# A four-layer graph attention kernel: the last layer's output stores move from SyncE's queue to ScalarE's

## The chip, the cores and the metric

The kernel runs on one core of a Trainium2 chip. The metric is the time of one execution on the device in microseconds (us). The core has five engines with a queue of instructions each: TensorE (PE, its weight loads shown apart as PEld), VectorE (DVE), ScalarE (ACT), GpSimd (POOL) and SyncE (SP). A transfer (DMA) is issued by one of these queues and then carried by the core's 16 DMA engines. A queue runs its instructions in order: one that waits holds up everything behind it.

## The reference

Four layers follow one another. Each adds the result of a graph attention to its input and normalises every row. There are 4096 nodes with 256 features; the adjacency matrix is random with density 1/256, plus the diagonal. The first three layers take a softmax over each row's neighbours. The last one, which the change touches, takes two:

```python
h = x @ W                                           # layer 3
e = leaky_relu(h @ a[:256] + (h @ a[256:]).T, 0.2)
att = softmax(where(adj > 0, e, -1e12), axis=1)
neg = -softmax(where(adj > 0, -e, -1e12), axis=1)
new = concatenate([att @ x, neg @ x], axis=1) @ fc_W
x = layernorm(x + elu(new))                         # the output
```

## The kernel before

The rows are worked in tiles of 128, so a layer has 32 tiles. A first part of the program turns each tile's adjacency into 13 lists of at most 128 neighbour nodes and a mask for each list. A layer then needs no full matrix: for each tile POOL gathers 13 blocks of 128 rows of `vals` (here: the features, already multiplied by the halves of `fc_W`, and two logarithms of attention terms) by index, `G<-vals,idx` at L645. The fourteenth block is the tile's own rows. It needs no index and comes by SP's queue: `G<-vals` at L642. A block is 128 x 516 floats, 258 KB.

A tile is worked in two halves of seven blocks (`RowTile.half`, L649). In layer 3 a half is: seven Relus on ACT that add the row's and the neighbours' terms (L686), an exponential (L687), its product with the mask on DVE (L688), a second exponential from the same Relus (L689), its product with the mask (L690), and 28 matrix products on PE (L723) that add into two banks. The own-row block belongs to the first half, at its seventh place (`FRONT = 6`).

Four of the 32 tiles, number 28 to 31, are worked densely against all nodes (`whole_rows`, L948): ACT makes the attention terms `pw` (L985, L987, L989), DVE masks them (L990), PE multiplies them by blocks `vw` (L993). This work is cut into units that are strewn between the halves of the 28 other tiles. It makes two passes over the nodes, one for each softmax; the second begins at about 1930 us.

`half_with_whole` writes one step of this weave: half a tile, then in the first half of tile m the finish of tile m-1, then some units of dense work. `finish` (L1060) reads the two banks: `positive` (L1050) scales the first with a reciprocal (L1054 on DVE, L1057 on ACT, giving `z`), L1074 to L1082 add the second, the elu's exponential (L1080 on ACT) and the old row `y`. `norm` (L1015) takes mean and variance (L1022, L1023), the reciprocal root by a chain of small DVE instructions (L1031 to L1041), and scales `y` (L1043). `GROUPS` says that the 28 gathered tiles are normalised alone and the four dense ones together. A tile's row block `y` is loaded by SP (`load_x`, L1012) into one of nine buffers, is changed in place, and is stored from the same buffer (L1045). A new `y` that takes the buffer waits until the store has landed.

The order on each engine is fixed when the program is built. A scheduler places the instructions by its own estimate of times; `issue_after(ins)` makes what is written inside it stand behind `ins`. So SP's queue in layer 3 holds, in a fixed order: a tile's row terms `S` (L635), its masks `mk` (L637), a finished row block's store (L1045), the own-row block of a coming tile (L642), its `y` (L1012), and the dense work's `vw` and `mw` (L970, L968). Buffers of `G` come from two pools of 16 and 14, shared by all tiles.

The end of the program is `close` with no following layer: what is left of the dense work, and the finish of the last tile.

Of the kernel before, what the change touches and what calls it, by code (L numbers as in the profile page):

```python
# [44 lines left out]
AF = mybir.ActivationFunctionType  # L45
# [5 lines left out]
P = 128  # L51
# [129 lines left out]
class Turns:  # L181


    def __init__(self, pools):
        self.pools = list(pools)
# [418 lines left out]
class RowTile:  # L604
# [44 lines left out]
    def half(self, half):  # L649
        L, n, nc = self.layer, self.layer.n, self.layer.nc  # L650
        prog, sh, S = L.prog, L.shared, self.S
        H, Wd, V, T, A = HEADS[n], WIDTH[n], VALS[n], TERMS[n], LOGS[n]
        if self.accs is None:
            pool = prog.ptwo[1 if n == 3 and self.step % 2 else 0]
            self.accs = [prog.bank(pool) for _ in range(2 if n == 3 else 1)]
        accs = self.accs
        G = [self.place(half * HALF + k) for k in range(HALF)]
        mh = self.mk[:, half * HALF:(half + 1) * HALF, :]
        if n < 2:

            if prog.masks is None:
                prog.masks = prog.bank(prog.pmask)
            there = prog.masks[:, half * BANK // 2:half * BANK // 2 + HALF * P // 4].bitcast(I32)
            nc.vector.tensor_scalar(there.rearrange("p (t i) -> p t i", t=HALF),
                                    mh.rearrange("p t i -> p (t i)").bitcast(I32)
                                    .rearrange("p (t i) -> p t i", t=HALF)[:, :, :P // 4], 0, None,
                                    op0=ALU.bitwise_or)
            mh = there.bitcast(U8)
            mh2 = mh.rearrange("p (o i) -> p o i", o=1).to_broadcast([P, 2, HALF * P])
        else:  # L670
            mh = mh[:, :, :P]
        pairs = [prog.wp.tile([P, 2, HALF, P], F32, name="w") for _ in range(H // 2)]
        w = [pair[:, k] for pair in pairs for k in range(2)]
        if n < 2:
            w = [w[1], w[2], w[3], w[0]]
        def masked(pair):

            pair = pair.rearrange("p h t i -> p h (t i)")
            nc.vector.scalar_tensor_tensor(pair, pair, LEAST, mh2, op0=ALU.max, op1=ALU.mult)  # L679

        def d(k, h):
            return G[k][:, V + T + h:V + T + h + 1]

        if n == 3:
            for k in range(HALF):
                nc.scalar.activation(w[0][:, k, :], S[:, 0, :], AF.Relu, bias=d(k, 0))  # L686
            nc.scalar.activation(w[1], w[0], AF.Exp, scale=-1.0)  # L687
            nc.vector.tensor_tensor(w[1], w[1], mh, op=ALU.mult)  # L688
            nc.scalar.activation(w[0], w[0], AF.Exp, bias=sh["shift2"])  # L689
            nc.vector.tensor_tensor(w[0], w[0], mh, op=ALU.mult)  # L690
            heads = (1, 0)
        else:
            for h in range(A, T):
                k = 0
                while k < HALF:
                    pos = half * HALF + k
                    e = 2 if pos % 2 == 0 and k + 1 < HALF else 1
                    if e == 2:
                        dd = self.slots[pos // 2][:, :2 * ROW[n]].rearrange("p (t c) -> p t c", t=2)
                        nc.vector.tensor_tensor(  # L700
                            w[h][:, k:k + 2, :], S[:, h:h + 1, :].to_broadcast([P, 2, P]),
                            dd[:, :, V + T + h:V + T + h + 1].to_broadcast([P, 2, P]), op=ALU.mult)
                    else:
                        nc.vector.tensor_scalar(w[h][:, k, :], S[:, h, :], d(k, h), None, op0=ALU.mult)
                    k += e
            for h in range(A):
                for k in range(HALF):
                    nc.scalar.activation(w[h][:, k, :], S[:, h, :], AF.Exp, bias=d(k, h))  # L708
                if n == 2:
                    nc.vector.scalar_tensor_tensor(w[h], w[h], LEAST, mh, op0=ALU.max, op1=ALU.mult)  # L710
                elif h % 2 == 0:
                    masked(pairs[h // 2])
            heads = list(range(A, H)) + list(range(A))
        for h in heads:
            for k in range(HALF):
                pos = half * HALF + k
                how = dict(start=pos == 0 and (n == 3 or h == heads[0]), stop=pos == NP - 1, skip_group_check=True)
                v = G[k][:, h * Wd:(h + 1) * Wd]
                if n < 2:
                    nc.tensor.matmul(accs[0][:Wd, h * P:(h + 1) * P], v, w[h][:, k, :], **how)  # L720
                else:
                    a = accs[h][:, :Wd] if n == 3 else accs[0][:, h * Wd:(h + 1) * Wd]
                    nc.tensor.matmul(a, w[h][:, k, :], v, **how)  # L723
# [22 lines left out]
class Layer:  # L746
# [3 lines left out]
    def __init__(self, prog, n):  # L750
        self.prog, self.n, self.nc, self.shared = prog, n, prog.nc, prog.shared
        self.order = ORDER[n]
        self.count = len(self.order)
        self.tiles = {}
        self.loaded = set()
        self.units = self.whole_rows()
        self.total = len(WHOLE[n]) * NT * (1 if n < 3 else 2)
        self.used = self.ahead = 0
        self.nxt = self.middle = self.between = None
        self.stored = []  # L760
        self.group = []
        self.ready = []
        self.step = 0
        self.last = ()
# [7 lines left out]
    def load(self, m, half):  # L772
        if m < self.count and (m, half) not in self.loaded:
            self.loaded.add((m, half))
            self.tile(m).load(half)
# [63 lines left out]
    def half_with_whole(self, m, part):  # L839

        projs = []
        self.step = 2 * m + part

        able = sorted((e for e in self.ready if e[0] < self.step), key=lambda e: e[2] >= MIX)
        self.set_banks()

        over = self.used == self.total and m > self.count - 4
        for entry, banks in zip(able, (self.prog.banks, self.prog.pthree)[:1 + over]):
            self.ready.remove(entry)
            projs.append(Projection(self.prog, self.n + 1, self.nxt, *entry[1:], banks=(banks,) * 3))  # L850
            projs[-1].transpose()
        with ExitStack() as order:
            for ins in self.last:
                order.enter_context(self.prog.tc.issue_after(ins))
            self.last = ()
            if part == 1 or self.tile(m).accs is None:
                self.tile(m).half(part)
        if self.between is not None:

            self.last = self.between()  # L860
            self.between = None
        for proj in self.stored:
            proj.store()
        for proj in projs:
            proj.copy()
            proj.multiply()
        if part == (0 if self.n == 3 else 1) and m >= 1:
            self.tile(m - 1).finish()
        self.whole(2 * m + part)
        for proj in projs:  # L870
            proj.row()
            proj.edge()
        self.stored = projs

    def steps(self):
        for m in range(self.count):
            for part in range(2):
                self.part(m, part)
# [10 lines left out]
    def close(self, following):  # L889
# [16 lines left out]
        if WHOLE[self.n]:  # L906
            for _ in self.units:
                pass
            if following is None:
                self.tile(last).finish()  # L910
                return


# [101 lines left out]
    def norm(self, y, m):  # L1015


        nc, ep = self.nc, self.prog.ep
# [22 lines left out]
            nc.vector.tensor_tensor(r, r, u, op=ALU.mult)  # L1041
        for i, (y, m) in enumerate(self.group):
            self.scaled = nc.vector.tensor_scalar(y, y, mv[:, i, 0:1], r[:, i:i + 1], op0=ALU.subtract, op1=ALU.mult)  # L1043
            dst = self.prog.out if self.n == 3 else self.shared["x"][self.n + 1]
            nc.sync.dma_start(out=dst[m * P:(m + 1) * P, :], in_=y)  # L1045
            if self.n < 3:
                self.ready.append((self.step + 1, y, m))
        self.group = []

# [38 lines left out]
def dense_layers(ctx: ExitStack, tc: tile.TileContext, ins: dict, out: bass.AP, ident):  # L1088
# [361 lines left out]
    def layer(nodes, following):  # L1450
        n = nodes.n
        nxt = following() if following is not None else None
        for blk in range(NB):
# [13 lines left out]
            else:  # L1467
# [6 lines left out]
                for it in range(BT):  # L1474
# [8 lines left out]
                    nc.vector.scalar_tensor_tensor(yt, z, 0.0, yt, op0=ALU.max, op1=ALU.add)  # L1483
                    nc.vector.scalar_tensor_tensor(yt, e, -1.0, yt, op0=ALU.add, op1=ALU.add)
            norm(y)
            dst = out if n == 3 else xD[n + 1]
            nc.sync.dma_start(out=to_tiles(dst[blk * W:(blk + 1) * W, :]), in_=y)
# [57 lines left out]
```

## Time and profile before

| | us |
|---|---|
| median of three executions (2258.48 to 2261.46) | 2259.3 |
| the execution that was profiled | 2261.27 |
| its span, from first to last instruction | 2259.5 |
| layer 3 in it, from about | 1764 |
| POOL's last gather ends | 2226.33 |
| last store issued | 2253.70 |
| mean granted TensorE clock | 0.963 |

Over the span PE is busy 89%, DVE 79%, ACT 77%, POOL 66%. In the 500 us of layer 3 (window 1760 to 2260) the costliest groups are L723 on PE (356.6 us), the gathers L645 on POOL (340 of them, 350.6 us), the Relus L686 on ACT (378, 132.2 us), L993 on PE (111.1 us) and the two mask products L688 and L690 on DVE (58.8 and 58.7 us). The 32 stores of the output are issued between 1813.0 and 2253.7, 0.338 us each at the median.

A line of the chain of waits is "start, length, engine and line". A line of the waits is "engine, line and what it writes <- what it waited for: us in total, times, longest". SPq is the queue of SP, whose instructions here are all transfers. A group of instructions has its count after x, then busy us and mean ns, then the engine's idle time before its members and what ended it.

### The profile page before, as it was taken

The page shows a single profiled execution, that of the slowest core. Times are in us where ns is not written, and L with a number is a line of the kernel's source. Part 1 is how long each engine was busy: PE and PEld are TensorE (multiplying, and loading weights), DVE is VectorE, ACT ScalarE, POOL GpSimd, SP SyncE. Part 2 cuts the span into 40 slices and gives each one's busy share as a digit, 9 for nine tenths or more (in the row PEclk, how much of TensorE's full clock was granted, in tenths as well). Part 3 has the DMA queues.
Part 4 walks back from the last instruction along what each step waited for, and adds up shares of the span by engine and source line. Part 5 has one row for each costly group of instructions (what it writes and reads, how often), then busy time and mean ns, then how long its engine had stood idle before and what let it go on. Part 6 is the DMA issues. An engine that isn't in the chain of part 4 may idle for free. (4 is left out here: it accounts for less than half of the span.)

```text
span 2259.5 us, 49108 instructions
## 1 busy us (share of the span) xinstructions
PE 2020.2 (89%) x15689; PEld 1842.9 (82%) x15689; DVE 1786.0 (79%) x5061; ACT 1730.1 (77%) x4977; POOL 1493.1 (66%) x1596
## 2 busy tenths in 40 slices
PE   4878888989999969989889898999998999899995
PEld 2658878878899859988889798999997888788784
DVE  2888999999999859888889786887976466655566
ACT  4777988988789859978889767987875666666653
POOL 2107656656667777777777777777773477777773
PEclk7898999999999979999999999999999999999998
DMA  8779868776567666666666666778777688898874
GB/s 283 250 242 357 281 214 255 251 245 225 147 169 193 178 197 171 180 179 168 175 182 168 171 166 182 211 216 235 227 220 212 197 281 273 261 284 261 260 239 122
DMA packets 250319, 492.99 MB, mean 218 GB/s; under 512 B 44385, under 2 KB 156610, under 8 KB 249666
## 3 DMA queue, kind: packets, MB, share of 16 engines
q0 software_dynamic: 81536, 245.30, 38.4%
q1 hardware_dynamic: 168514, 244.46, 33.7%
q8 instruction: 126, 2.06, 0.4%
q14 instruction: 143, 1.17, 0.2%
HBM read 437.05 MB, written 52.54 MB: 217 GB/s over the span
## 5 line engine op out<-in xcount | busy, mean ns | idle before, releaser
L645 POOL DMA_INDIRECT G<-vals,idx x1456 | 1480.1, 1017 | 723.2 <-issue 225.1
L708 ACT ACTIVATE w<-S,G 128x128 f32<-128x128 f32 x3248 | 1000.1, 390 | 137.9 <-DMA G<-vals,idx 99.6
L720 PE MATMUL bank<-w,G 128*65 128x128 f32 x7168 | 840.7, 277 | 61.0 <-DVE w L679 61.0
L720 PEld LDWEIGHTS bank<-w,G 128*65 128x65 f32 x7168 | 801.9, 141 | 70.8 <-DVE w L679 69.5
L679 DVE SCALAR_TENSOR_TENSOR w<-w,bank 128x1792 f32<-128x1792 f32 x256 | 514.7, 2014 | 16.6 <-ACT w L708 14.2
L723 PE MATMUL bank<-G,w 128*128 128x257 f32 (+1 forms) x2688 | 495.7, 342 | 33.7 <-ACT z L1057 21.6
L723 PEld LDWEIGHTS bank<-G,w 128*128 128x128 f32 x2688 | 436.0, 195 | 82.7 <-ACT z L1057 26.1
L993 PE MATMUL bank<-vw,pw 128*128 128x129 f32 (+1 forms) x2048 | 301.2, 304 | 1.8 <-issue 1.8
L993 PEld LDWEIGHTS bank<-vw,pw 128*128 128x128 f32 x2048 | 276.4, 193 | 17.8 <-issue 2.3
L686 ACT ACTIVATE w<-S,G 128x128 f32<-128x128 f32 x392 | 137.2, 391 | 148.6 <-DMA G<-vals 94.6
L438 DVE TENSOR_SCALAR oh<-iota,place 128x256 bf16<-128x256 f16 (+2 forms) x992 | 222.6, 300 | 9.7 <-PE bank L444 9.7
L700 DVE TENSOR_TENSOR w<-S,G 128x256 f32<-128x256 f32 x384 | 152.4, 417 | 69.9 <-DMA G<-vals,idx 66.8
L444 PE MATMUL bank<-mk,oh 128*128 128x132 fp8e4 x2336 | 191.3, 227 | 15.6 <-DVE oh L438 9.3
L555 PE MATMUL bank<-wext,xT 128*128 128x268 f32 (+3 forms) x640 | 180.8, 416 | 15.6 <-ACT xT L546 12.8
L444 PEld LDWEIGHTS <-oh 128*128 128x128 bf16 x2336 | 147.6, 99 | 51.0 <-DVE oh L438 16.2
L383 ACT ACTIVATE mk<-raw 128x1024 uint8<-128x1024 int32 x128 | 130.5, 1051 | 29.6 <-DMA raw<-in_adjB_dram 29.6
L555 PEld LDWEIGHTS bank<-wext,xT 128*128 128x128 f32 x640 | 119.6, 204 | 35.4 <-ACT xT L546 15.6
L983 DVE SCALAR_TENSOR_TENSOR pw<-pw,mw 128x512 f32<-128x512 f32 x192 | 127.4, 689 | 18.0 <-ACT pw L982 17.7
L982 ACT ACTIVATE pw<-Sw,d 128x512 f32<-128x512 f32 x192 | 133.0, 709 | 8.6 <-PE bank L993 5.5
L688 DVE TENSOR_TENSOR w<-w,mk 128x896 f32<-128x896 f32 x56 | 61.0, 1090 | 96.3 <-ACT w L687 87.6
L710 DVE SCALAR_TENSOR_TENSOR w<-w,mk 128x896 f32<-128x896 f32 x80 | 86.7, 1087 | 39.8 <-ACT w L708 39.6
L451 ACT ACTIVATE cm<-bank 128x396 uint8<-128x396 f32 (+1 forms) x160 | 69.0, 452 | 47.4 <-PE bank L444 46.3
(130 smaller groups left out, 1519.3 us busy)
## 6 DMA issues: line engine op xcount, KB each, us to landing
raw<-in_adjB_dram SPq DMA_DIRECT2D x128, 512.0 KB
mk<-maskC SPq DMA_DIRECT2D x112, 231.0 KB
G<-vals,idx POOLq DMA_INDIRECT x1456
S<-edge SPq DMA_DIRECT2D x64, 256.0 KB
vw<-vals SPq DMA_DIRECT2D x96, 129.0 KB
xp<-y SPq DMA_DIRECT2D x96, 128.0 KB
y<-xp SPq DMA_DIRECT2D x96, 128.0 KB
mw<-maskW SPq DMA_DIRECT2D x20, 528.0 KB
```

Source lines behind the costliest of these rows:

```text
L438: nc.vector.tensor_scalar(oh[:, :n * P], iota[:, :n * P], self.place[:, it, j:j + 1], None, op0=ALU.is_equal)
L444: nc.tensor.matmul(accs[b][:, s * MC:(s + 1) * MC], oh[:, (k - a) * P:(k - a + 1) * P], mk[:, j, it, :].bitcast(FP8), start=touches[b][0] ...
L555: nc.tensor.matmul(pp[:, :c1 - c0], self.xT[:, k, :], wext[:, k, c0:c1], start=(k == 0), stop=(k == KT - 1 and brow is None))
L645: nc.gpsimd.indirect_dma_start(out=self.place(pos), out_offset=None, in_=sh["v"][n][:NODES[t], :], in_offset=bass.IndirectOffsetOnAxis(ap= ...
L679: nc.vector.scalar_tensor_tensor(pair, pair, LEAST, mh2, op0=ALU.max, op1=ALU.mult)
L686: nc.scalar.activation(w[0][:, k, :], S[:, 0, :], AF.Relu, bias=d(k, 0))
L700: nc.vector.tensor_tensor(w[h][:, k:k + 2, :], S[:, h:h + 1, :].to_broadcast([P, 2, P]), dd[:, :, V + T + h:V + T + h + 1].to_broadcast([P ...
L708: nc.scalar.activation(w[h][:, k, :], S[:, h, :], AF.Exp, bias=d(k, h))
L720: nc.tensor.matmul(accs[0][:Wd, h * P:(h + 1) * P], v, w[h][:, k, :], **how)
L723: nc.tensor.matmul(a, w[h][:, k, :], v, **how)
L982: nc.scalar.activation(p, S[:, h], AF.Exp, bias=d)
L993: nc.tensor.matmul(accs[it][:, c:c + Wd], p[:, it, :], v[:, c:c + Wd], start=(j == 0 and h == heads[0]), stop=(j == NT - 1), skip_group_ch ...
```

## The change

The store leaves `norm` for layer 3. There the pair of buffer and tile number is put into a list `outs` instead. `store_rows` empties the list with transfers that ACT issues. It is called in `half_with_whole` behind the next half tile, with an order that puts the stores behind that half's second exponential (L689, recorded as `exps`), and in `close` ahead of the last tile's finish and behind it. The other layers keep their stores on SP. Nothing that is computed changes: 32 stores of 128 KB leave from another queue. In the built program SP loses these 32 transfers and keeps the order of the rest; ACT has them behind L689, in some halves behind one or two Relus of the half after; PE's and POOL's order stays; a few ACT and DVE instructions near the second dense pass and in the last tiles change places.

```diff
--- before.py
+++ after.py
@@ -686,7 +686,7 @@
                 nc.scalar.activation(w[0][:, k, :], S[:, 0, :], AF.Relu, bias=d(k, 0))
             nc.scalar.activation(w[1], w[0], AF.Exp, scale=-1.0)
             nc.vector.tensor_tensor(w[1], w[1], mh, op=ALU.mult)
-            nc.scalar.activation(w[0], w[0], AF.Exp, bias=sh["shift2"])
+            self.exps = nc.scalar.activation(w[0], w[0], AF.Exp, bias=sh["shift2"])
             nc.vector.tensor_tensor(w[0], w[0], mh, op=ALU.mult)
             heads = (1, 0)
         else:
@@ -759,6 +759,7 @@
         self.nxt = self.middle = self.between = None
         self.stored = []
         self.group = []
+        self.outs = []
         self.ready = []
         self.step = 0
         self.last = ()
@@ -855,6 +856,11 @@
             self.last = ()
             if part == 1 or self.tile(m).accs is None:
                 self.tile(m).half(part)
+                if self.outs:
+                    order.enter_context(self.prog.tc.issue_after(self.tile(m).exps.ins))
+                    self.store_rows()
         if self.between is not None:
 
             self.last = self.between()
@@ -871,6 +877,11 @@
             proj.row()
             proj.edge()
         self.stored = projs
+    def store_rows(self):
+        for y, m in self.outs:
+            self.nc.scalar.dma_start(out=self.prog.out[m * P:(m + 1) * P, :], in_=y)
+        self.outs = []
 
     def steps(self):
         for m in range(self.count):
@@ -907,7 +918,9 @@
             for _ in self.units:
                 pass
             if following is None:
+                self.store_rows()
                 self.tile(last).finish()
+                self.store_rows()
                 return
 
 
@@ -1041,9 +1054,10 @@
             nc.vector.tensor_tensor(r, r, u, op=ALU.mult)
         for i, (y, m) in enumerate(self.group):
             self.scaled = nc.vector.tensor_scalar(y, y, mv[:, i, 0:1], r[:, i:i + 1], op0=ALU.subtract, op1=ALU.mult)
-            dst = self.prog.out if self.n == 3 else self.shared["x"][self.n + 1]
-            nc.sync.dma_start(out=dst[m * P:(m + 1) * P, :], in_=y)
-            if self.n < 3:
+            if self.n == 3:
+                self.outs.append((y, m))
+            else:
+                nc.sync.dma_start(out=self.shared["x"][self.n + 1][m * P:(m + 1) * P, :], in_=y)
                 self.ready.append((self.step + 1, y, m))
         self.group = []
```

## The prediction

> **What bounds the kernel now.** I read first the groups of instructions of layer 3's stretch (1760 to 2260 us) and its waits, then the list of POOL's instructions, then the chain of waits of the last 60 us, because the change touches nothing before layer 3: the listing of instructions by engine shows layers 0 to 2 unchanged.
>
> From the groups and the waits (line, what was waited for: us in total, times, longest):
>
> ```profile
> L645 POOL DMA_INDIRECT G<-vals,idx x340 | 350.6, 1031 | 130.9 <-PE bank L723 41.5 <-issue 26.2 <-DMA vals<-row 22.9
> ACT w L686 <- DMA G<-vals: 94.6, 17, 8.6
> POOL G L645 <- PE bank L723: 41.5, 121, 3.8
> SPq L1045 <- DVE y L1043: 120.1, 25, 22.5
> SPq L1012 <- DMA out_dram<-y: 63.9, 23, 7.5
> ```
>
> The lines seem to offer much: ScalarE waits 94.6 us for own-row blocks (`G<-vals`, no index), and SP's queue stands 120.1 us at the store, in front of those blocks. But a wait is worth only what the pace-setter gets of it. POOL's list shows that every gather follows the last after 0.30 us, whoever is named as the releaser (41.5 us in 121 times is mostly this 0.30 us), from 1788.66 to 2226.33, with two larger gaps only: 0.73 at 1802.50 and 1.05 at 1956.77. Over that stretch its 327 gathers take 337.2 us and 100.8 us lie between them: 1.34 us from start to start, so 13 gathers, one tile, take **17.4 us**. PE needs less. It is full from 1800 to 1930, catching up, and does 602 matmuls there in 130.0 us, 0.216 each; a tile's 56 L723 and 16 L993 are then **15.6 us**:
>
> ```profile
> 1800.00:1930.00 130.00, 130.00 (x602) 114.20 (x601) 82.27 (x248) 88.20 (x186) 99.71 (x99) 1.00 0.87 271
> 2030.00:2200.00 170.00, 159.59 (x721) 137.41 (x720) 96.53 (x289) 103.33 (x223) 131.60 (x127) 0.99 0.83 255
> ```
>
> (us, then busy PE, PEld, DVE, ACT, POOL, clock, DMA share, GB/s.) From 2030 PE has holes, 10.4 us of 170: it is ahead and waits for blocks. So POOL's issue sets the pace of the loop, and behind its last gather comes a tail of 33.2 us (2226.33 to 2259.5) in which nothing is overlapped with gathers. The tail's chain:
>
> ```profile
> 2203.70 0.42 DVE y L1043
> 2204.14 0.34 SPq L1045
> 2204.65 7.64 DMA G<-vals
> 2212.31 0.70 ACT w L686 x2
> ...
> 2235.26 1.00 DVE w L688
> 2236.39 1.00 DVE w L690
> 2239.12 1.35 DVE y L1043 x4
> 2240.84 0.48 ACT z L1057
> ...
> 2246.66 0.41 DVE y L1043
> 2247.44 0.48 ACT z L1057
> ...
> 2253.26 0.41 DVE y L1043
> ```
>
> Here the store does count: the own-row load of the second last tile stands on SP behind the store at 2204.14, lands at 2212.3, and ScalarE has waited 8.56 us for it. PE is idle from 2209 to 2216.5 (0.02 us busy of 7.5), then DVE is full to 2240.
>
> **What the skill says.** The Trainium skill, "DMA: Bandwidth & Descriptors", section "Issuing engines are not separate DMA queues": transfers issued by ScalarE, SyncE or GpSimd end on the same 16 engines, and another issuer saves sequencer time only. So no bandwidth is won; the trace agrees in so far as the shares above (0.83 to 0.87) belong to all issuers together. "Perfetto Trace Analysis", section "DMA Instruction — HWDGE (DVE, Sync)": the wait for a semaphore is held by the issuing sequencer. The trace agrees: SP stands at L1045 for 120.1 us, and the loads behind stand with it. After the change ScalarE will stand so. The same page, section "GPSIMD Instruction", says to time GpSimd by start-to-start spacing; here that is 1.34 us against a mean reported 1.03.
>
> **The change, part by part.**
>
> *Removed from SP:* 32 stores, 0.34 us each (L1045, median 338 ns), and their wait for L1043. Behind each stands the next tile's own-row load, and sometimes the next mask. In 2047 to 2170 these loads were issued every 17.5 us; with only the wait for `S` (L635) or `mk` (L637) ahead of them they could come 1.7 to 3.7 us earlier. ScalarE then starts that half earlier, PE too. The gain in the loop is 0, because POOL's gathers are 0.30 us apart already: PE only waits later, at a gather's landing. What covers it is POOL; if that cover weren't there, the 10.4 us of 2030 to 2200 would be the prize (rival A).
>
> *Kept on SP:* `y<-xp` (L1012) reuses a stored row's buffer and still waits for that store's landing (63.9 us). The store now goes out somewhat later, so this wait grows; behind it stand `vw` and the next `S`. In the chain one such load, at 2173.75, ended in a DVE wait of 7.4 us at L688. Estimate for the loop: 0, it is behind POOL; up to +2 if a late `S` reaches a gather's buffer.
>
> *Added on ScalarE:* 32 issues. No row shows an issue on ScalarE; SP's 0.34 us is the nearest and I take it (between 0.1 and 0.7). 32 x 0.34 = 10.9 us on an engine that is busy 283.6 of 460 us. Each also waits for its L1043: at 2116.46 L689 ends, L1043 at 2118.4, so ScalarE stands 1.9 us; behind it stand the next half's Relus, whose own-row block landed only at 2123.8, and `pw` (L985). The cover is ScalarE's wait of 5.5 to 6.3 us there. If the earlier block takes that cover away, some 2 us a tile lie on ScalarE, which has 17.4 − 10.7 = 6.7 us free per tile: still 0 for the pace.
>
> *The pass change* (1925 to 1957, where the dense block's second pass starts): there the listing puts a store ahead of L985 and L989, their L990 on DVE ahead of the last pass's reciprocal. Exposed: about 0.62 + 0.53 + 0.69 = 1.8 us, less 1.65 that the own-row load at 1925.45 gains. Net +0.1 on POOL's gap at 1956.77; bounds −0.75 (the gap down to 0.30) and +1.5.
>
> *The tail.* The second last tile's block can go out near 2190 (its buffer is free, no store ahead). Its half 0 then starts with its last gather: issued by 2199.29, landing some 5.3 us later as those at 2202.01 and 2203.35 did, at 2204.6 instead of 2212.3, −7.7 us. Half 1 of that tile and half 0 of the last follow on gathers that end at 2208.68 and 2217.00, and DVE no longer runs full behind them. The next bound is the last half: its last gather ends 2226.33, lands at 2229.5 to 2230, then L686 0.4, L687 0.95: L688 at 2231.2 to 2231.9 instead of 2235.26, **−3.3** (−4.1 at best). From there the 18 us to the last L1043 are one serial chain on DVE, unchanged but for four store issues on ScalarE ahead of `z` at 2240.84: 4 x 0.34 less the 1.3 in which ScalarE waits anyway, +0.15 (up to +1.2 with 0.6 us an issue). The final store leaves right after its L1043 as before.
>
> Sum: 0 + 0.1 − 3.3 + 0.15 = **−3.0 us** on the profiled execution, 2261.27 to 2258.2. That execution lies 2.0 above the median of the three (2259.3); I carry the difference over: **2256.4**.
>
> **The rivals.**
> *A: the stall is won back in full.* PE's holes in 2030 to 2230 (18 us) close and the tail shortens too. For it: ScalarE's 94.6 us. Against it: POOL's 0.30 us between gathers. It needs gathers that issue faster once blocks are freed earlier, for instance if the long ones are waits within (327 gathers at the usual 0.95 us would be 28 us less than the 337.2). −8 to −15 us, near 2248. Chance 0.12.
> *B: slower; ScalarE stands at the store and POOL runs out of buffers.* ScalarE is the only engine through which every block passes. If a store's wait grows to over 6 us (DVE late behind L690 of the half whose exponentials ScalarE has just finished), the Relus behind it free blocks late, PE falls behind POOL's 17.4 us, and POOL waits. The point is ScalarE's 6.7 us of free time a tile; 0.3 us past it in 20 tiles is 6 us: about 2265. The pass change's +1.5 and issues of 0.7 us add to it. For it: the waits at 1.9 us are many; against it: PE has 1.8 us of slack a tile besides. Chance 0.20.
> *C: nothing.* `y<-xp`'s wait takes the place of the store's on SP, or the second last tile's block waits for something else, or DVE stays the tail's bound. About 2259.3. Chance 0.16.
> That the stores do not move can be left out: the listing shows all 32 on ScalarE.
> My forecast, the tail shorter by 1.5 to 5 us, has 0.52.
>
> **How the numbers follow.** A measurement of this kernel can tell about 0.2% from no change, 4.5 us: below 2254.8 or above 2263.8. Faster: A's 0.12 and a fifth of the forecast, 0.22. Slower: most of B, 0.17. Same: the rest, 0.61. The forecast and C together reach from 2253.5 to 2260.5; for 8 in 10 I take in the near parts of A and B, 2250.5 to 2265.
>
> **What would show it.** Right: POOL's gathers still 0.30 us apart and ending near 2226 in the profile after; own-row loads issued right behind `S` or `mk`; ScalarE's wait for `G<-vals` well under 94.6; PE no longer idle in 2209 to 2216; L688 of the last half 3 us earlier, and 30 us from POOL's last gather to the end. Wrong: POOL's last gather moved by more than 1.5 us (down is A, up is B); waits of POOL over 0.30 us; or the tail still 33 us long (C).

## The result and the profile after

The change is faster by a little: the ratio of its time to that of before is 0.9979, 95% interval [0.9969, 0.9989], from 11 executions of each on the same chips (medians 2258.1 and 2261.46 us). The profiled execution took 2258.1 us, its span is 2256.3; the prediction's sum for it was 2258.2. The number on record was 2256.4, for the median.

Line numbers move by 13 or 14 in the kernel after: the store is L883 on ScalarE, the scaling of `y` is L1056 (was L1043), `z` L1071 (L1057), the load of `y` L1025 (L1012). Of layer 3's stretch, 1760 to 2260 us, these are the waits of the engines and then of SP's queue:

```profile
ACT w L686 <- DMA G<-vals,idx: 74.6, 83, 6.6
...
POOL G L645 <- PE bank L723: 38.8, 115, 4.1
...
ACT w L686 <- DVE y L1056: 31.4, 15, 4.0
...
ACT w L686 <- DMA G<-vals: 11.2, 6, 4.0
```

```profile
SPq L1025 <- DMA out_dram<-y: 136.7, 23, 14.0
SPq L635 <- ACT w L686: 125.8, 23, 9.8
```

One more line of before belongs beside them, ScalarE's wait for the gathers by index:

```profile
ACT w L686 <- DMA G<-vals,idx: 39.0, 41, 6.6
```

ScalarE's wait for own-row blocks has gone from 94.6 us to 11.2. Most of it has only moved. ScalarE now stands 31.4 us at the stores ("<- DVE y L1056": the Relu behind the store shows the wait, because an issue isn't counted as work), and its wait for gathers by index has grown from 39.0 to 74.6 us; the three together fell from 133.6 to 117.2. SP's wait for a store to land before `y` is loaded has grown from 63.9 to 136.7 us. Of the span, 3.2 us are gone. The reason stands in POOL's instructions: in this profile every gather of the stretch from 1787.6 to 2227.7 follows the last after 0.30 to 0.32 us. POOL's 38.8 us for PE don't speak against that: one of these waits is the 4.09 us ahead of 1786.39, and the other 114 are the same 0.30 us as everywhere. The two larger gaps of before (0.73 and 1.05 us) are gone.

The chain of waits from the last gathers on is where the time went. Times are start and length:

```profile
2226.42 0.30 issue
2226.73 3.72 DMA G<-vals,idx
2230.47 0.41 ACT w L686
2230.90 0.96 ACT w L687
2231.88 1.09 DVE w L688
2233.11 1.00 DVE w L690
2236.62 1.03 DVE y L1056 x3
2237.80 0.37 DVE y L1056
2238.46 0.40 ACTq L883
2238.91 0.48 ACT z L1071
...
2244.73 0.41 DVE y L1056
2245.57 0.48 ACT z L1071
...
2251.38 0.41 DVE y L1056
```

In before this chain ran through a store on SP and an own-row block that landed at 2212.3. Here it runs through the last gather, which lands at 2230.45, and the last half's L688 starts at 2231.88 instead of 2235.26. SP's list shows why; the last two own-row loads stand behind no store, and the first of them goes out at 2187.48, 17 us earlier than before (x2: both, the second only when its buffer was free):

```profile
2186.99 0.32 SPq L1025 DMA_DIRECT2D y<-xp  x1
2187.48 11.62 SPq L642 DMA_DIRECT2D G<-vals  x2
```

Put side by side, the two profiled executions differ by this sum from the last half's L688 on (us; the ends of the tail are the points of the chain):

| step | before | after | difference |
|---|---|---|---|
| start of the last L688 | 2235.26 | 2231.88 | −3.38 |
| from there to the end of the four scalings | 5.21 | 6.29 | +1.08 |
| from there to `z` of the second last tile | 0.37 | 0.74 | +0.37 |
| from `z` to the last scaling's start | 12.42 | 12.47 | +0.05 |
| from the last scaling's start to the end of the span | 6.24 | 4.92 | −1.32 |
| sum | | | −3.20 |

Two rows of it were not in the prediction: +1.08 and −1.32. The experiments take them up. Counted from the end of POOL's last gather (2226.33 in before, 2227.67 here), the tail fell from 33.2 to 28.6 us, which is 4.5 us; POOL's last gather came 1.3 us later in this execution.

### The profile page after: what moved, and what is told of

It reads as the page before. It is cut to its first block, busy times and chain, and to the rows that moved or that the text cites. A ratio compares the mean times of both kernels' runs of the same rounds, so it can differ in the third digit from the quotient of the medians.

```text
span 2256.3 us, 49117 instructions
## 1 busy us (share of the span) xinstructions
PE 2022.0 (90%) x15689; PEld 1841.6 (82%) x15689; DVE 1790.3 (79%) x5061; ACT 1737.1 (77%) x4977; POOL 1488.7 (66%) x1596
## 5 line engine op out<-in xcount | busy, mean ns | idle before, releaser
L720 PE MATMUL bank<-w,G 128*65 128x128 f32 x7168 | 840.0, 277 | 56.5 <-DVE w L679 56.3
L720 PEld LDWEIGHTS bank<-w,G 128*65 128x65 f32 x7168 | 800.5, 140 | 66.9 <-DVE w L679 65.4
L688 DVE TENSOR_TENSOR w<-w,mk 128x896 f32<-128x896 f32 x56 | 61.1, 1092 | 66.6 <-ACT w L687 65.1
L1003 DVE TENSOR_TENSOR pw<-pw,mw 128x512 f32<-128x512 f32 x64 | 43.5, 690 | 86.8 <-ACT pw L1002 45.7
```

## The experiments

The theory under test is the prediction's: POOL's issue sets the pace, so that the own-row loads' new freedom is worth nothing in the loop, and the gain is that of the last two own-row loads. The rivals are that the loop's loads bring the gain (A, "loop theory"), and that ScalarE's stand at the stores costs time that the tail's gain covers (B).

A word on the chips. The kernels ran on five of them. On two (one for `three` and `drop_before`, one for `dense_sp`) before takes 2260 to 2261 us, on the other three 2752 to 2757. Each ratio is taken on one chip, so all of them stand; but the slower chips are another machine for this question, as the kernel `one` below shows.

### Is POOL the pace-setter? One gather fewer per tile, in the kernel before

```diff
-        s = pos // per
+        s = (min(pos, NP - 2) if n == 3 else pos) // per        # place()
...
+            if n == 3 and pos == NP - 1:                        # load()
+                continue
```

> The kernel before without the thirteenth gather of each tile in layer 3: the last block is the twelfth's once more, so the last neighbour list is left out of the sums, PE, ScalarE and DVE do as much as before, and a tile uses 13 buffers, not 14. If POOL's issue sets the loop's pace (1.34 us a gather), 26 gathers in the window go and layer 3 ends some 20 to 26 us earlier, up to PE's own need (it was idle for about that long after 1930). If the own-row load behind the store set the pace of before (loop theory), gathers are not the limit and the gain is under 8 us.

Measured: 2233.31 beside 2261.36 us, ratio 0.9868 [0.9851, 0.9885] from four executions: 30 us less by the ratio, 28 by the medians. That is more than the 20 to 26 us expected; 28 gathers left the window, not 26. The busy time by stretch (us; PE, PEld, DVE, ACT, POOL, clock, DMA share, GB/s) says how far it went, first in before and then in this kernel:

```profile
1930.00:2030.00 100.00, 91.94 (x407) 79.19 (x406) 63.67 (x191) 70.40 (x150) 76.40 (x76) 0.97 0.89 276
```

```profile
1930.00:2030.00 100.00, 98.95 (x457) 86.41 (x456) 61.67 (x186) 67.75 (x152) 76.69 (x77) 1.00 0.88 280
...
2170.00:2200.00 30.00, 29.98 (x138) 25.77 (x137) 21.36 (x79) 18.11 (x43) 21.40 (x20) 1.00 0.74 216
```

PE, idle for 8 us of the first stretch in before, is busy for 98.95 of 100, and for 29.98 of the last 30 before POOL's last gather, which ends at 2197.2 instead of 2226.3. Between them PE has 5.3 us of holes in 140, and POOL waits there for PE to free a buffer, up to 4.7 us at a time: the pace has passed to PE in part. From the gather behind POOL's first gap to its last one it is 413.6 us (1783.56 to 2197.2), where before has 443.5 (1782.83 to 2226.33): 29.9 us less. The tail behind is longer here, 37.7 us instead of 33.2, so that the span of this execution, the slowest of the four, is 24.6 us shorter. ScalarE's wait for own-row blocks has hardly changed, since every store still stands on SP in front of them (in this kernel the Relu is L688):

```profile
ACT w L688 <- DMA G<-vals: 86.1, 18, 8.1
```

So in before the gathers set the pace, and the own-row waits were spare time: 30 us went while 86.1 of the 94.6 us stayed. The loop theory had under 8 us here; it falls. What the experiment can't tell apart is POOL's issuing and the transfer behind it: each gather left out is also 258 KB less for the DMA engines. For the question of this document it makes no difference. (A tile also uses 13 buffers instead of 14 in this kernel; POOL didn't wait for buffers in before either, apart from the two gaps of the prediction, so that isn't what explains 30 us.)

### Three stores instead of 32

Only the stores of tiles 23, 26 and 27 go by ScalarE; 23 is the one that stands on SP in front of the last two own-row loads.

```diff
-            if self.n == 3:
+            if self.n == 3 and m in (23, 26, 27):
                 self.outs.append((y, m))
             else:
-                nc.sync.dma_start(out=self.shared["x"][self.n + 1][m * P:(m + 1) * P, :], in_=y)
-                self.ready.append((self.step + 1, y, m))
+                dst = self.prog.out if self.n == 3 else self.shared["x"][self.n + 1]
+                nc.sync.dma_start(out=dst[m * P:(m + 1) * P, :], in_=y)
...
```

> Only the stores of tiles 23, 26 and 27 by ScalarE; tiles 0 to 22, 24, 25 and the four dense tiles stay on SP. Three terms of the tail are meant: the last two own-row loads stand behind no store (L688 of the last half near the landing of the last gather, 3 to 3.5 us earlier than in before), the last store is ScalarE's (4.5 us from its issue to the end, not 5.8), and the dense group's stores aren't ahead of the last two z on ScalarE, nor its small DVE steps behind L688 (5.2 us from the last L688 to the end of the four scalings, not 6.3). Tail theory: 4 to 5 us under before, ratio 0.9975 to 0.9985, 1 to 1.5 us better than the change. Loop theory: a tenth of the change's gain. If the gain needs all three, this is the best version.

Measured: 2256.49 beside 2261.36 us, ratio 0.9983 [0.9972, 0.9993]. That is 3.8 us by the ratio, with an interval that the change's own overlaps widely; whether it is 1 to 1.5 us better than the change, as expected, these intervals can't tell. The waits and the chain of this kernel:

```profile
ACT w L686 <- DMA G<-vals: 68.4, 16, 6.4
POOL G L645 <- PE bank L723: 43.5, 130, 4.2
```

```profile
2231.57 1.09 DVE w L688
2232.80 1.00 DVE w L690
2235.52 1.35 DVE y L1056 x4
2237.25 0.48 ACT z L1073
...
2243.06 0.41 DVE y L1056
...
2249.71 0.41 DVE y L1056
```

This is the plainest reading of the case. ScalarE still waits 68.4 of the 94.6 us for own-row blocks, with every store of the loop on SP, and the kernel is about as fast as the change. The last L688 is at 2231.57, 3.7 us earlier than in before; the last scaling starts 3.6 us earlier, and the end of the span is 2254.7, 5.0 us after that instead of 6.2. So against the profile of before tile 23's store is worth 3.6 us and the last store some 1.3. Twenty-nine of the moved stores were not needed for the gain.

### The four kernels on the slower chips: which stores bring it?

All are the change with another condition in the same line as above: `m == 23` (`one`), `m < 23` (`loop`), `m >= 23` (`tail`), and in `no_tie` the list and the tie are left out:

```diff
-                self.outs.append((y, m))
+                nc.scalar.dma_start(out=self.prog.out[m * P:(m + 1) * P, :], in_=y)
```

> The kernel before with a single store moved: that of tile 23, which stands on SP's queue ahead of the last two own-row loads, is issued by ScalarE behind the next half's second exponential; the other 31 stay on SP. Tail theory (the gain is the last two own-row loads, freed from the store ahead of them): L686 of the second last tile starts near 2206 instead of 2212, the last half's L688 near 2232 instead of 2235.26, and most of the change's gain, 2 to 4 us (ratio 0.998 to 0.999). Loop theory (the gain is earlier own-row loads in all tiles): a twenty-eighth of it, within 0.3 us of before. If the end after the last store depends on the issuing queue (5.8 us in before from SP, 4.5 us in after from ScalarE), this kernel shows 5.8 us, since its last store is SP's.

> The stores of tiles 0 to 22 by ScalarE as in the change; those of tile 23 to 27 and of the dense block by SP as before. Tail theory: no gain, within 1 us of before (ratio 0.9995 to 1.0005), POOL's last gather ends within 1.5 us of 2226.3, and the second last tile's own-row block again lands late, near 2212. Loop theory: most of the change's gain, 3 us or more. If ScalarE's stand at the stores costs time (rival B), this one is slower than before by 1 to 3 us, the cost that the tail's gain hides in the change.

> The stores of tiles 23 to 27 and of the dense block by ScalarE, those of tiles 0 to 22 by SP as before. Tail theory: as fast as the change, 3 to 5 us under before. Loop theory: within 1 us of before. Rival B: faster than the change by what ScalarE's stand costs in the loop, 1 to 3 us. POOL's last gather should end near 2226.3 as in before; in the change it ended at 2227.7.

> All 32 stores on ScalarE, without the tie: each stands where the scheduler puts it when it is written, behind its L1043. Tail theory: the own-row loads are as free on SP as in the change, POOL sets the pace, so the time is the change's within 1 us if the store's place on ScalarE is no worse. If ScalarE's stand matters (rival B), the store waits for L1043 ahead of more of the half's Relus and exponentials, and this is slower than the change by 2 to 8 us, with POOL's gaps over 0.30 us or a longer tail to show it.

`one`, `loop` and `no_tie` were run again, on further chips of the slower kind, where these expectations for the faster kind say little:

> As the kernel of the label loop, on a chip on which the kernel before takes some 2260 us and not 2757. Tail theory: within 1.5 us of before (ratio 0.9995 to 1.0005); POOL's last gather ends within 1.5 us of 2226.3; the second last tile's own-row block lands near 2212, ScalarE's wait for own-row blocks in the rest of the loop falls under 40 us and buys nothing. Loop theory: 3 us or more faster. Rival B: 1 to 3 us slower.

> As the kernel of the label one (tile 23's store alone on ScalarE), on a chip on which the kernel before takes some 2260 us. Tail theory: ScalarE's wait for own-row blocks stays at 70 us or more in the loop, the last half's L688 comes 3 to 4 us earlier than in before, the last store to the end takes 5.8 us; 2.5 to 4 us under before (ratio 0.9982 to 0.9989). Loop theory: no gain.

> As the kernel of the label no_tie (all stores on ScalarE, placed behind their L1043 by the scheduler), on a chip on which the kernel before takes some 2260 us. Tail theory: as the change, 2 to 5 us under before; POOL's gaps stay 0.30 us. Rival B: slower than the change by 2 to 8 us.

> Once more the stores of tiles 0 to 22 by ScalarE and the other nine by SP. Tail theory, on a chip on which before takes some 2260 us: within 1.5 us of before (ratio 0.9995 to 1.0005), POOL's last gather within 1.5 us of 2226.3, tile 26's own-row block landing near 2212. Loop theory: 3 us or more faster. Rival B: 1 to 3 us slower. On a chip on which before takes some 2755 us the interval is too wide for that, and only the trace counts.

> Once more tile 23's store alone by ScalarE. Tail theory, on a chip on which before takes some 2260 us: 2.5 to 4 us under before (ratio 0.9982 to 0.9989), ScalarE's wait for own-row blocks still 65 us or more, the last half's L688 3 to 4 us earlier than 2235.26, 5.8 us from the last store to the end. Loop theory: no gain.

Measured (all with before at 2752 to 2757 us):

| stores by ScalarE | ratios with 95% intervals |
|---|---|
| tiles 0 to 22 | 0.9996 [0.9981, 1.0010], 1.0003 [0.9986, 1.0020], 0.9999 [0.9982, 1.0015] |
| tile 23 | 0.9994 [0.9973, 1.0015], 1.0003 [0.9981, 1.0024], 1.0016 [1.0000, 1.0032] |
| tiles 23 to 31 | 0.9984 [0.9967, 1.0002] |
| all, no tie | 1.0008 [0.9986, 1.0029], 0.9997 [0.9976, 1.0019] |

The loop's stores bring nothing and cost nothing that three runs can see, as the tail theory has it. But tile 23's store alone brings nothing either, where 2 to 4 us were expected; that expectation missed. All stores without the tie, which were to be as fast as the change, show no gain either; the intervals are too wide to exclude one. The nine last stores have 0.9984, within the 3 to 5 us expected, with 1 still inside the interval. The profile of `one` says what is different. In its list of groups the first line is

```profile
L645 POOL DMA_INDIRECT G<-vals,idx x1456 | 1461.6, 1004 | 1234.5 <-issue 420.8 <-ACT w L708 227.0 <-PE bank L720 154.2
```

The gathers' idle time in front that nothing in the profile explains ("issue") is 420.8 us, and was 225.1 in before on a faster chip; for PE's L720 it is 205.0 us, where the page of before names no such part. The mean granted clock is 0.888 and not 0.963. What holds the engines up there the profile doesn't show. Layers 0 to 2 are some 440 us longer, and in layer 3 the own-row blocks are hardly late: ScalarE waits 14.7 us for them in `one`, with the loop's stores on SP, and 94.6 in before on a faster chip. The same goes for the last two: in `loop`, where the last two own-row loads do stand behind tile 23's store, SP's list and ScalarE's list read

```profile
2690.46 0.34 SPq L1061 DMA_DIRECT2D out_dram<-y  x1
2690.97 7.59 SPq L642 DMA_DIRECT2D G<-vals  x2
```

```profile
2696.90 0.69 ACT L686 ACTIVATE w<-S,G 128x128 f32<-128x128 f32 x2 [0.58 <-DMA G<-vals]
```

ScalarE has waited 0.58 us for that block, where it waited 8.56 us in before on a faster chip. What the store held up was not needed earlier. So these runs don't speak against the tail's mechanism; they show that the wait that it removes can be absent on another chip, and with it the gain. They can't tell small effects apart either: single executions there reach from 2736 to 2776 us. The change itself was not run on these chips, nor tile 23's store alone on a faster one.

What can be read from every trace is the time from the last store's issue to the end of the span, since it depends on no cover: 5.8 to 6.0 us where SP issues it (before and all runs of `one` and `loop`; 6.4 in `drop_before`), and 4.5 to 4.7 us where ScalarE does (the change, `three`, `tail`, `no_tie` and the last kernel below). That is the −1.32 of the table. No run shows what fills it.

### The change with the dense tiles' stores back on SP

```diff
-            if self.n == 3:
+            if self.n == 3 and m < 28:
```

> The change with the four dense tiles' stores back on SP, in their old place: 28 stores by ScalarE. Tail theory: from the start of the last L688 to the end of the four scalings 5.3 us (as in before and in the kernel of three stores), not 6.3 (as in the change); z follows 0.4 us behind them and not 0.7; so 1.4 us better than the change, as fast as the kernel of three stores, 4 to 6 us under before where before takes some 2260 us. If the 23 loop stores by ScalarE cost time (rival B), it stays 1 to 3 us behind the kernel of three stores (2256.5 beside a before of 2261.4). Loop theory: no better than the change.

Measured: 2254.37 beside 2259.78 us, ratio 0.9976 [0.9966, 0.9987], on the chip where before takes 2260. That is as good as or a little better than the change, within the intervals of both. But one step of the expectation is wrong, as DVE's list shows:

```profile
2230.03 1.09 DVE L688 TENSOR_TENSOR w<-w,mk 128x896 f32<-128x896 f32 x1
2234.75 1.06 DVE L1056 TENSOR_SCALAR y<-y,mv,b 128x256 f32<-128x256 f32 x3
2235.92 0.41 DVE L1056 TENSOR_SCALAR y<-y,mv,b 128x256 f32<-128x256 f32 x1
```

From the start of L688 to the end of the scalings it is still 6.3 us, not 5.3. So the dense stores were not the reason. The traces show two orders of the same instructions. In before and in `three`, ten small steps of the last two norm chains (L1031 to L1039) stand ahead of the last L688 on DVE; in the change and in `dense_sp` only the first does, and the rest come between and behind L688 and L690. On ScalarE, four of the last half's Relus stand behind the dense tiles' last `z` in the first two kernels and only three in the others, so that `z`, and with it the chains, waits for one more gather to land (in the change that Relu, at 2227.53, had waited 0.86 us for its gather; `z` is at 2227.84).

The first of these looks larger than it is. In before the ten steps take 1.0 us ahead of L688; behind it they take their time all the same, only on the other side of the line from which the table counts. From the last mean and variance (L1023) to the end of the scalings it is 6.2 us in before and 6.3 in `three`, 6.4 in `dense_sp` and 6.6 in the change. From POOL's last gather to the end of the scalings it is 9.5 us in `three` and 10.5 in the other two, and 0.6 to 0.8 of this 1.0 us is there before the last mean and variance end. So the second order costs about 1 us of the tail, and most of it fits the later place of `z`; no run changes one of the two alone.

It was the scheduler that chose, by its own estimate. From L688 to the scalings 6.3 us appear in the change, `tail`, `no_tie` and `dense_sp`, where the stores of tiles 24 and 25 are ScalarE's, and 5.2 to 5.3 in before, `one`, `loop` and `three`, whose stores of tiles 24 and 25 are SP's. But `drop_before`, which moves no store, has 6.5 and the second order too. What tips it was not tried.

The other half came as expected: `z` follows the scalings after 0.2 us and not 0.7. Of the four stores that stand ahead of it in the change, three are dense tiles' and one is tile 25's. (A gathered tile that ends while dense tiles wait for their group closes the group: tile 25 is normalised with two of them, and the last dense tile alone.)

On rival B this kernel is the better test, since it holds 28 stores on ScalarE against `three`'s three, on the same kind of chip: 0.9976 against 0.9983. By the two intervals a cost of the loop's stores over about 2 us isn't there; a smaller one can't be excluded.

## Why the prediction was right

**The pace.** "The gain in the loop is 0, because POOL's gathers are 0.30 us apart already" held, and `drop_before` shows it by the other side: one gather fewer per tile is worth 30 us with the own-row waits untouched. Of the 83 us by which ScalarE's wait for own-row blocks fell, none shows in the time from one gather to the next. From the gather behind layer 3's first gap to the end of the last it is 443.5 us in before, 441.3 in the change, 445.0 in `three` and 442.9 in `dense_sp`, in no order that follows the stores. A small correction: in before, two of POOL's gaps were more than 0.30 us, 1.2 us together over it, and they are gone in the change. They are gone in `three` as well, which leaves the loop's stores on SP, so they are not the change's gain but differ between executions.

**The pass change.** Estimated at +0.1, bounds −0.75 and +1.5. The L688 that follows it starts at 1949.44 and not 1950.04, although layer 3's first gap on POOL ended 3.6 us later in this execution (1786.39, 1782.83 in before); the gap of 1.05 us has closed to 0.30. That looks like the lower bound, −0.75, but the gap has closed in `three` as well, so it can't be credited to the moved stores. What can be said is that they cost POOL nothing here: a store does stand ahead of L985 (now L998), at 1940.14, in a wait of ScalarE of 4.11 us that the profile puts down to PE, and no gap of POOL came of it.

**The tail's start.** Predicted 2231.2 to 2231.9 for L688, −3.3; measured 2231.88, −3.4, in a profile whose last gather ended 1.3 us later than in before. The two errors cancel: the last gather landed 2.8 us after its issue's end, not 3.2 to 3.7. That the figure is met so closely is luck in this. Half 0 of the second last tile began 5.3 us earlier, at 2206.97, not 7.7, and PE's hole of 7.8 us from 2209 shrank to 5.6 us from 2205.6 instead of closing; neither mattered, since the last gather came later still.

**ScalarE's stores ahead of `z`.** Predicted +0.15, "up to +1.2" (its own terms, 4 x 0.34 less 1.3, give +0.06); measured +0.37. The issues take 0.34 us each as estimated from SP's row (median 338 ns for both queues), and the four together 1.82 us, overlapped with the scalings that they wait for.

**What was missing.** "From there the 18 us to the last L1043 are one serial chain on DVE, unchanged" is the step that failed: the stretch is 19.5 us in the change. The chain doesn't begin at L688. It holds norm steps too, of which ten stood ahead of L688 in before and nine of these stand behind it now, and they wait for a `z` that has moved on ScalarE. The cause is the scheduler's order. The part on the change names it ("a few ACT and DVE instructions ... in the last tiles change places"), but the sum has no term for it. And the end after the last store, taken as it was, is 1.3 us shorter when ScalarE issues that store. The two nearly cancel, so that the sum came out right for the profiled execution (2258.1, predicted 2258.2) with two terms missing: to a tenth, that is luck. In place of "30 us from POOL's last gather to the end" it is 28.6.

**The rivals.** A's mark, POOL's last gather moved down, didn't come; B's, waits over 0.30 us, neither: ScalarE's stand was at most 4.0 us a time, under the 6.7 us of free time that the prediction took as the point from which it decides. C's half came: SP's wait for `y` has doubled, to 136.7 us, and none of the engines' waits names the rows `y` that it held up. The ratio over all executions, 4.7 us by the point value, is somewhat more than the −3.0 of the sum, and its interval, 2.5 to 7.0 us, holds it. It is near the 4.5 us by which the tail became shorter. The number on record, 2256.4 (its own terms give 2256.2), started from a median of three executions of before, 2259.3; the median of eleven is 2261.5, so the difference of 2.0 that it carried over was not there.

## What to carry to other kernels

A wait of 94.6 us on a busy engine was worth nothing in the loop, because another engine's instructions stood 0.30 us apart nearly from the first to the last; look for the engine without gaps before you price a stall, and take work from it to test it. What a freed queue can win is then at the ends, where that engine has stopped: here two own-row loads behind one store, and the last store itself, so that moving three stores does as much as moving 32. And when a build-time scheduler places the instructions, compare its order line by line on every engine, also where the edit has no instruction: another order of a few steps on ScalarE and DVE took back about 1 us of the tail.

## What was not expected of the hardware

The span ended 4.5 to 4.7 us after the last store's issue when ScalarE issued it, and 5.8 to 6.4 us after when SP did, on both kinds of chip. And three of the five chips ran the same program some 22% slower than the other two (before at 2752 to 2757 us against 2260 to 2261). In `one`, on such a chip, the idle time ahead of POOL's gathers that no wait explains is 420.8 us; in before on a faster chip it is 225.1.
